# First wave of quantized weights gathered inside the chip's memory in a macaron + S4 kernel

## The chip, the cores and the metric

The kernel runs on one core of one Trainium2 chip. The metric is device time in microseconds (us): the median of three runs of the kernel before is 2035.08 us (2033.29 to 2036.26).

## The reference

The input `u` has 2048 rows of 1024 numbers in float32 (2 sequences of 1024). Three residual blocks follow one another:

```python
x = x + 0.5 * ffn(layernorm(x))
x = x + s4(layernorm(x))
x = x + 0.5 * ffn(layernorm(x))
# ffn, the same weights both times:
h = silu(xf @ Wg) * (xf @ Wu)     # 1024 -> 2752
out = h @ Wd                      # 2752 -> 1024
# each W is dequantized from 4 bits, eight rows of W to a 32-bit word:
w = (w4[k, n] - (z4[k // 128, n] + 1)) * s[k // 128, n]
```

A group is 128 rows of a weight matrix that share a row of zero points and a row of scales; the 1024 rows have eight groups.

## The kernel before, in words

**Work and order.** The tokens go in four blocks of 512. Block and layer make eight jobs (`JOBS`). In each job `gate_up` runs eight waves (`WAVES`), and each of the first five waves makes three blocks of 128 columns of gate and of up at once, in six banks of PSUM (`pg`). A wave takes eight steps, one for each group `g`. A step has twelve products of 512 columns on PE: the weights of the group (`w_up`, float32 made from signed bytes) times a high part `xTh` and a low part `xTl` of the turned input, for each of the six banks. After each step but the last of a wave, each bank is multiplied by the ratio of this group's scale to the next's (`rat`), by ScalarE (ACT, line 811) or VectorE (DVE, line 815): a rescale. The next step adds to the bank, and so waits for it. Steps are numbered through the job: wave 0 is steps 0 to 7, and step 8 is the first of wave 1.

**Weights.** Dequantizing is done once, in job 0. A wave's words (`raw`) are fetched, split into two words of four nibbles each by DVE (`even`, `raw`), added to the zero points spread as bytes, and turned into eight planes of signed bytes (`q`). Plane `j` holds every eighth row of the weights: rows `8r + j`. The planes are written to DRAM (`w_q`), and from there `load_bytes` (line 764) reads a group of 128 rows to the chip (`b`), four steps ahead of use; `make_weights` (line 781) turns it into float32, three steps ahead, on GpSimd (POOL, line 788) for all of wave 0.

**Wave 0** cannot hide this. `first_split` makes its planes. DVE unpacks the zero words (line 351 in eight pieces, line 360 spreads them as `z_w`), and splits the words (lines 591 to 597). POOL makes the odd planes (line 605), ACT the even ones (line 607). Of each plane, the 16 rows of group 0 go from chip to chip into `first_tile` (line 609: eight transfers of 12 KB). The whole planes go to DRAM in four transfers (`keep`, line 613), and groups 1 to 7 are read back from there (line 772).

**The input's first rows.** In `start`, ACT and DVE take the moments of the 512 rows, POOL the power -1/2 (line 205), and DVE refines it (lines 218 to 224). `first_rows` normalizes in pieces: columns 0 to 127, 128 to 511, 512 to 1023, tiles 0 and 2 on DVE, 1 and 3 on ACT. `first_turn(c)` turns column block `c` on PE (four transposes, `pt`) and splits it: ACT copies (line 1829 or 1833), then DVE (1830) or POOL (1834, 1835) makes the low part. Block 0 is turned ahead of step 0, block `c` by step `c`.

**What sets the order.** The instructions of an engine run in the order in which a scheduler put them. `in_order_of_writing` ties those of a stretch of code, on the engines named, to the order in which they were written. Hooks (`at(up, s, f)`) put a piece of work at step `s`, or with `.5` at half of it. Every DMA is issued by an engine's queue (SP, ACT or POOL) in that engine's order, and waits there for its data. `first_weights` (line 716) plans the making of waves 1 to 7 by hooks: at which step a piece of the split (`split`), a plane (`dequantize`, line 660) and a write to DRAM (`keep_bytes`, line 674) go.

**The scales.** `scales_in_pieces` turns rows of scales on PE (`ps_s`), copies them on ACT (line 422), guards them on POOL (lines 425 to 427), inverts them on DVE (line 429) and makes `rat` on POOL (lines 433, 434): for units 0 to 5 in `start`, for units 6 to 17 from step 4 on, and for 18 to 29 from step 6 on.

Of the kernel before, what the change touches and what calls it, by code (L numbers as in the profile page):

```python
# [9 lines left out]
F32 = mybir.dt.float32  # L10
# [47 lines left out]
def macaron_s4_kernel(  # L58
# [270 lines left out]
    def zero_words(which):  # L329

        if which:
            n = HID // 8 // SEGD
            z = t2("zq_1").bitcast(I32)[: GD * SEGD, :n]
            nc.sync.dma_start(z, down_qz.rearrange("g (s n) -> (g s) n", s=SEGD))
            return z
        n = INTER // 8 // SEG
        z = t2("zq_0").bitcast(I32)[:, :n]
        for i, src in enumerate((gate_qz, up_qz)):
            own = slice(GK * SEG * i, GK * SEG * (i + 1))
            nc.scalar.dma_start(z[own], src.rearrange("g (s n) -> (g s) n", s=SEG))  # L340
        return z
# [4 lines left out]

    def unpacked_zeros_in_pieces(tab, z, zi):
# [12 lines left out]
        nc.vector.tensor_scalar(  # L360
            tab.bitcast(U16).rearrange("p (n k) -> p n k", k=2),
            zi.unsqueeze(2).to_broadcast([p, 8 * n, 2]),
            -8.0 * 257,
            120.0 * 257,
            ALU.mult,
            ALU.add,
        )

# [179 lines left out]

    first_tile = bpool.tile([P, width_of(0)], I8, tag="b", name="b_0_0")
    minus_128 = const.tile([P, 1], F32, tag="minus_128", name="minus_128")  # L550
# [7 lines left out]
    def fetch_in_pieces(w, queues=(nc.sync, nc.sync)):  # L558

        raw = t4(f"raw_{w}").bitcast(I32)[:, : width_of(w)]  # L560
        packed[w] = [raw, None]
        for own, i, lo, hi in columns(w):
            queues[i].dma_start(raw[:, own], (gate_qw, up_qw)[i][:, lo:hi])
            yield
# [8 lines left out]
    def first_zero_words():  # L573

        n = width_of(0) // 8
        z = t2("zq_first").bitcast(I32)[:, :n]
        for queue, (own, i, lo, hi) in zip((nc.sync, nc.scalar), columns(0)):
            own = slice(own.start // 8, own.stop // 8)
            src = (gate_qz, up_qz)[i][:, lo // 8 : hi // 8]
            wide = src.unsqueeze(1).to_broadcast([GK, 16, own.stop - own.start])  # L580
            queue.dma_start(z[:, own], wide)
        return z

    def first_split(zq):
# [4 lines left out]
        raw = packed.pop(0)[0]  # L589
        unpacked_zeros(z, zq, zi)  # L590
        nc.vector.tensor_scalar(even, raw, 3, NIBBLES, ALU.logical_shift_left, ALU.bitwise_and)
# [8 lines left out]
        def dequantize(j):  # L600
            pair = pairs.setdefault((j % 2, j // 4), t2(f"q_0_{j}").bitcast(I8)[:, : 2 * n])
            q = pair.rearrange("p (a n) -> p a n", a=2)[:, j // 2 % 2, :]
            view = lambda a, dt: a.bitcast(dt).rearrange("p (n k) -> p k n", k=4)[:, j // 2, :]
            if j % 2:
                nc.gpsimd.tensor_copy(q, view(raw, I8))
            else:
                nc.scalar.activation(q, view(even, U8), AF.Identity, bias=minus_128)
            queue = nc.scalar if j == 6 else nc.sync
            queue.dma_start(first_tile[j:P:8], q[: P // 8])

        def keep(odd, half, queue):
            rows = w_q[0].rearrange("(r b a two) n -> two b r a n", b=2, a=2, two=2)[odd, half]
            queue.dma_start(rows, pairs[odd, half].rearrange("p (a n) -> p a n", a=2))

        return dequantize, keep

# [43 lines left out]
    def dequantize(w, j):  # L660

        n = width_of(w)
        if w not in unpacked:
            q = ypool.tile([P, 4 * TB], F32, tag="y", name=f"q_{w}").bitcast(I8)[:, : 8 * n]
            unpacked[w] = q.rearrange("p (two a n) -> p two a n", two=2, a=4)
        q, src = unpacked[w][:, j % 2, j // 2, :], packed[w][j % 2][:, j // 2, :]
        if w == 1 and j % 2 == 0:
            nc.scalar.activation(q, src.bitcast(U8), AF.Identity, bias=minus_128)
        else:
            nc.gpsimd.tensor_copy(q, src)  # L670
        if j == 7:
            packed.pop(w)

    def keep_bytes(w, odd):
        rows = w_q[w].rearrange("(r a two) n -> two r a n", a=4, two=2)[odd]
        nc.sync.dma_start(rows, unpacked[w][:, odd])

    def fetch_down(a, rt):
# [37 lines left out]
    def first_weights(up, dn, at):  # L716
# [3 lines left out]
        for w in range(1, len(WAVES)):  # L720
            s0 = (0, 4, 8 * w - (14 if w < 5 else 15))[min(w, 3) - 1]
            steps = (0.5, 1, 2.5, 3, 3) if w == 1 else range(6)
            in_pieces(at, [(up, s0 + d) for d in steps], lambda w=w: split(w))
            copies = {1: (3, 3, 3.5, 3.5) + (3.5,) * 4, 2: (3, 3, 4, 4, 5.5, 5.5, 6, 6)}
            copies = copies.get(w, (3, 3, 4, 5, 6, 6, 7, 8))
# [3 lines left out]
            for k, d in zip(EVEN_FIRST, copies):  # L729
                at(up, s0 + d, lambda w=w, k=k: dequantize(w, k))  # L730
            for odd, o in enumerate({1: (3.5, 3.5), 2: (5.5, 7)}.get(w, (6.5, 9.5))):
                at(up, s0 + o, lambda w=w, odd=odd: keep_bytes(w, odd))
# [59 lines left out]
    def next_weights():  # L792
# [4 lines left out]
        for k in range(MAKE) if i == 0 else ():  # L797
            make_weights(k)
        if i + LOAD < len(queue):
            load_bytes(i + LOAD)  # L800
        if i + MAKE < len(queue):
            make_weights(i + MAKE)
        return made.pop(i)


# [11 lines left out]
    def gate_up(j, b, hooks):  # L817
        hi, lo = pieces[b]
        ps = {}
        for s, (wi, g) in enumerate(STEPS):  # L820
# [20 lines left out]
            if j == s == 0:  # L841
                turns = [(1 - k, pos, done) for k, pos, done in turns]
            for i, (k, pos, done) in enumerate(turns):
                if i == len(order):
                    for hook in hooks.get(s + 0.5, ()):
# [20 lines left out]
                if g < GK - 1:  # L866
# [730 lines left out]
    def fast():  # L1597
# [5 lines left out]
        for j, (b, k) in enumerate(JOBS):  # L1603
# [88 lines left out]
            if j == 0:  # L1692
                rows = {}
                for s, f in ((0, lambda: fetch_zeros(1)), (1, lambda: fetch(2)), (2, lambda: fetch_zeros(2))):
                    at(up, s, pinned(f, ET.SP))
# [107 lines left out]
    def first_rows(t, lo, hi):  # L1803
# [39 lines left out]
    def start():  # L1843
# [10 lines left out]
        zeros_down = zero_words(1)  # L1854
        dequantize_first, keep_first = first_split(zq)
        second = fetch_in_pieces(1)
        for j in (1, 3, 5):
            dequantize_first(j)
        next(second)
        dequantize_first(7)  # L1860
        mv, scratch = first_moments()
        dequantize_first(0)
        first_scales = scales_in_pieces(0, 3, srow)
        next(first_scales)
        dequantize_first(2)
        next(first_scales)
        guess(0, 1, mv, LIFT)
        for _ in range(2):
            keep_first(1, _, nc.gpsimd)
        dequantize_first(4)  # L1870
        dequantize_first(6)
        keep_first(0, 1, nc.scalar)
        keep_first(0, 0, nc.sync)
        next(second)
        for _ in first_scales:
            pass
        keep_warm(10, scratch)
# [5 lines left out]
        for t in range(NT):  # L1883
            first_rows(t, 0, P)
        for t in (0, 1, 2):
            first_rows(t, P, 512)
        points = zero_points_in_pieces(0, zeros)
        for _ in range(4):
            next(points)
        first_turn(0)  # L1890
        for _ in range(5):
            next(points)
        first_rows(3, P, 512)
        for t in range(NT):
            first_rows(t, 512, HID)
        for _ in points:
# [93 lines left out]
```

## Time and profile before

| what | us |
|---|---|
| median of three runs | 2035.08 |
| the profiled execution's own time | 2036.95 |
| its span on the core | 2035.2 |
| PE busy in the span | 2004.1 |
| DVE, ACT, POOL busy | 1631.0, 1416.2, 1371.5 |
| first product of step 0 begins | 17.85 |
| the six `xTh` products of step 7 begin | 44.97 |
| the six `xTh` products of step 8 (wave 1) begin | 47.66 |

The span is the stretch of time from the first to the last instruction in the trace; the execution's own time is 1.75 us longer. All times within the run count from the span's start. PE's busy time is an average over all stages: after the first 45 us PE hardly waits, and what the change touches lies in those first 45 us. There the timeline, engine by engine, tells more than the page.

### The profile page before, as it was taken

What the parts mean: (1) busy time and instruction counts of PE and PEld (TensorE: products, weight loads), DVE (VectorE), ACT (ScalarE), POOL (GpSimd) and SP (SyncE); (2) the same over time, 40 slices, a digit from 0 to 9 for tenths busy, and PEclk for the clock granted to TensorE, in tenths of its full rate; (3) what the DMA queues carried; (4) which work ended last, traced back from release to release, by engine and by line L of the source; (5) the groups of instructions that cost most, each with busy time, mean ns of one, the idle gap of its engine ahead of it and who ended that gap; (6) DMA issues with size and microseconds to landing.
All of it is one profiled execution on the core that took longest, in us unless ns stands there. A gap on an engine that the chain in (4) does not pass through costs nothing.

```text
span 2035.2 us, 29665 instructions
## 1 busy us (share of the span) xinstructions
PE 2004.1 (98%) x9202; PEld 1374.5 (68%) x9202; DVE 1631.0 (80%) x2710; ACT 1416.2 (70%) x2221; POOL 1371.5 (67%) x1771
## 2 busy tenths in 40 slices
PE   7999999999999999999999999999999999999998
PEld 4656766577766677656866578667686676866576
DVE  8987878868888778877778777887878878777776
ACT  7888787747775577777767776764776647767775
POOL 6977868748765577655976578754686646965542
PEclk9999999999999999999999999999999999999999
DMA  5343332343524236311552126242263331661113
GB/s 166 119 136 99 110 103 62 79 103 92 148 63 102 73 71 196 120 30 35 143 161 85 33 50 172 79 93 83 50 161 93 84 90 38 160 187 34 35 37 102
DMA packets 345965, 197.13 MB, mean 97 GB/s; under 512 B 166989, under 2 KB 323670, under 8 KB 345798
## 3 DMA queue, kind: packets, MB, share of 16 engines
q1 hardware_dynamic: 344206, 192.55, 34.9%
q10 hardware_dynamic: 1464, 2.20, 0.3%
q8 instruction: 75, 1.23, 0.3%
q14 instruction: 92, 0.75, 0.1%
q0 software_dynamic: 128, 0.39, 0.1%
HBM read 127.52 MB, written 48.57 MB: 87 GB/s over the span
## 4 chain that ended last, share of the span: by engine, by line
PE 93%; DVE 3%; POOL 1%; issue 1%; ACT 1%; DMA 0%; ACTq 0%; POOLq 0%; DVEq 0%
PE pg L855 58%; PE po L949 30%; PE pc L1317 3%; PE pb L1317 1%; ACT pg L811 1%; DVE pg L815 1%; DVE po L815 0%; POOL w_up L788 0%; DVE rawd L629 0%; POOL r L205 0%; DVE hf L890 0%; POOL hl L897 0%; DVE rawd L632 0%; DVE stats L1797 0%; POOL q L670 0%
## 5 line engine op out<-in xcount | busy, mean ns | idle before, releaser
L811 ACT ACTIVATE pg<-pg,rat 128x512 f32<-128x512 f32 x1280 | 807.1, 661 | 383.6 <-PE pg L855 378.8
L815 DVE TENSOR_TENSOR pg<-pg,rat 128x512 f32<-128x512 f32 x1128 | 748.2, 692 | 146.5 <-PE pg L855 139.1
L855 PE MATMUL pg<-xTh,w_up 128*128 128x512 f32 x2752 | 844.4, 435 | 3.9 <-DVE pg L815 2.7
L855 PE MATMUL pg<-xTl,w_up 128*128 128x512 f16 x2752 | 708.0, 381 | 2.5 <-DVE pg L815 2.0
L855 PEld LDWEIGHTS pg<-xTh,w_up 128*128 128x128 f32 x2752 | 518.4, 189 | 167.5 <-DVE pg L815 7.7
L788 POOL CAST w_up<-b 128x768 fp32r<-128x768 int8 (+2 forms) x491 | 376.6, 773 | 356.9 <-PE pg L855 259.1
L811 ACT ACTIVATE po<-po,ratd 128x512 f32<-128x512 f32 x669 | 438.2, 662 | 145.3 <-PE po L949 144.6
L949 PE MATMUL po<-hl,w_down 128*128 128x512 f32 x1344 | 527.5, 393 | 3.5 <-DVE po L815 3.1
L949 PE MATMUL po<-hh,w_down 128*128 128x512 f32 x1344 | 523.4, 390 | 0.0
L815 DVE TENSOR_TENSOR po<-po,ratd 128x512 f32<-128x512 f32 x611 | 424.4, 696 | 112.1 <-PE po L949 111.2
L855 PEld LDWEIGHTS <-w_up 128*128 128x128 bf16 x2752 | 226.7, 98 | 340.2 <-issue 156.1
L788 POOL CAST w_down<-bd 128x512 fp32r<-128x512 int8 x352 | 217.8, 623 | 151.6 <-PE po L949 73.7
L949 PEld LDWEIGHTS po<-hl,w_down 128*128 128x128 f32 x1344 | 252.5, 188 | 64.0 <-DVE po L815 8.3
L949 PEld LDWEIGHTS po<-hh,w_down 128*128 128x128 f32 x1344 | 252.8, 188 | 51.3
L897 POOL TENSOR_TENSOR hl<-hf,hh 128x512 fp32r<-128x512 f32 x168 | 217.1, 1292 | 7.1
L896 POOL CAST hh<-hf 128x512 fp32r<-128x512 f32 x168 | 108.3, 645 | 81.1 <-DVE hf L890 62.3
L890 DVE SCALAR_TENSOR_TENSOR hf<-pg,rat,g 128x512 f32<-128x512 f32 x168 | 121.1, 746 | 40.5 <-ACT g L887 34.3
L887 ACT ACTIVATE g<-pg,rat 128x512 f32<-128x512 f32 x168 | 110.1, 688 | 33.7 <-PE pg L855 17.8
L1002 POOL TENSOR_TENSOR x<-x,yr 128x512 f32<-128x512 f32 x52 | 66.8, 1284 | 0.0
L291 POOL TENSOR_TENSOR lo<-x,hi 128x512 f16<-128x512 f32 x48 | 62.0, 1291 | 0.0
L189 DVE BATCH_NORM_STATS2 stats<-x 128x6 f32<-128x512 f32 x88 | 60.0, 681 | 0.0
L289 POOL TENSOR_TENSOR mid<-hi,top 128x512 bf16<-128x512 f32 x48 | 56.0, 1167 | 0.0
(214 smaller groups left out, 1081.2 us busy)
## 6 DMA issues: line engine op xcount, KB each, us to landing
b<-wq SPq DMA_DIRECT2D x319, 96.0 KB
bd<-wdq SPq DMA_DIRECT2D x336, 64.0 KB
x<-in_L_attn_u_dram SPq DMA_DIRECT2D x30, 512.0 KB
yz<-y SPq DMA_DIRECT2D x56, 256.0 KB
yr<-yz SPq DMA_DIRECT2D x56, 256.0 KB
b<-wq SPq DMA_DIRECT2D x128, 64.0 KB
sz<-xn SPq DMA_DIRECT2D x16, 512.0 KB
st<-sz SPq DMA_DIRECT2D x64, 128.0 KB
```

What stands on the lines that cost most here:

```text
L291: nc.gpsimd.tensor_tensor(lo[:, own], n[:, own], hi[:, own].bitcast(F32), ALU.subtract)
L788: nc.gpsimd.tensor_copy(t, b)
L811: nc.scalar.activation(dst, src, AF.Copy, scale=sc)
L815: nc.vector.tensor_tensor(dst, src, sc.to_broadcast(list(dst.shape)), ALU.mult)
L855: product = lambda: nc.tensor.matmul(p, weights, (lo, hi)[k][:, g, :], start=(g == 0 and not done), stop=(g == GK - 1 and done), skip_grou ...
L887: nc.scalar.activation(g, pg, AF.Silu, scale=rat[:, 2 * f, GK - 1 :])
L890: nc.vector.scalar_tensor_tensor(hf, pu, last, g, ALU.mult, ALU.mult)
L896: nc.gpsimd.tensor_copy(hi, hf)
L897: nc.gpsimd.tensor_tensor(lo, hf, hi.bitcast(F32), ALU.subtract)
L949: nc.tensor.matmul(ps[c], w[:, bass.ts(c, P)], part, start=(f == 0 and k == 0), stop=(f == NF - 1), skip_group_check=True,)
L1002: nc.gpsimd.tensor_tensor(part, part, rows_back.pop((a, t)), ALU.add)
L1317: nc.tensor.matmul(dst, lhsT, rhs, start=start, stop=stop, skip_group_check=True)
```

## The change

The order of instructions from step 9 or so on is the same on every engine; what differs lies ahead of it.

1. **Words by row, then group.** The words of wave 0 lie on the chip with row `r` of group `g` on partition `8r + g` (before: `16g + r`), and the zero words likewise. A plane's 128 partitions thus hold, for each `r`, the eight groups side by side, and one transfer puts them into partition `8r + j` of a tile `landed` (128 x 8 x 768 bytes): eight transfers of 96 KB, in place of eight of 12 KB, four of 192 KB to DRAM, and seven loads of 96 KB. Step 0's weights wait for all eight, and the other groups' for nothing more. `landed` is written to DRAM once, at step 3, for the later jobs.
2. **A plane to POOL, the zero words' last step to ACT.** Plane 0 is a `tensor_scalar` on POOL; the spread of the zero words (before: line 360 on DVE) is an `activation` on ACT.
3. **The rows' second halves** (columns 512 to 1023, four pieces) go from DVE and ACT to POOL, behind the first four `w_up`.
4. **Wave 1** keeps its planes in four tiles of their own (`landed` has the place of `q`), writes them in four transfers of 192 KB where two of 384 KB were, as each pair of planes is done, and spreads splits and planes over later steps. ACT's planes are tied to the order of writing among the rescales. The loads of steps 8 and 9, and `w_up` of step 8, are issued at step 5.5.
5. **Order at the start.** The guard of the scales goes behind the even planes; five pieces of the zero points ahead of the refinement; step 0 does its six `xTh` products ahead of the six `xTl` products, with block 1 turned after three; blocks 2 and 3 are turned half a step or a step later. Rescales are tied to the order of writing in steps 0 to 6. Three loads go from ACT's queue to SP's.

```diff
-            nc.scalar.dma_start(z[own], src.rearrange("g (s n) -> (g s) n", s=SEG))
+            nc.sync.dma_start(z[own], src.rearrange("g (s n) -> (g s) n", s=SEG))
...
-        nc.vector.tensor_scalar(
...
+        if on_act:
+            nc.scalar.activation(dst, src, AF.Copy, bias=120.0 * 257, scale=-8.0 * 257)
+        else:
+            nc.vector.tensor_scalar(dst, src, -8.0 * 257, 120.0 * 257, ALU.mult, ALU.add)
...
-    first_tile = bpool.tile([P, width_of(0)], I8, tag="b", name="b_0_0")
+    landed = ypool.tile([P, 4 * TB], F32, tag="y", name="landed").bitcast(I8)[:, : 8 * width_of(0)]
+    landed = landed.rearrange("p (g n) -> p g n", g=GK)
...
+            if w == 0:
+                src = src.rearrange("(g r) n -> r g n", g=GK)
...
-            if j % 2:
+            if j == 0:
+                nc.gpsimd.tensor_scalar(q, view(even, U8), -128.0, None, ALU.add)
+            elif j % 2:
                 nc.gpsimd.tensor_copy(q, view(raw, I8))
             else:
                 nc.scalar.activation(q, view(even, U8), AF.Identity, bias=minus_128)
             queue = nc.scalar if j == 6 else nc.sync
-            queue.dma_start(first_tile[j:P:8], q[: P // 8])
+            queue.dma_start(landed[j:P:8], q)
...
+    def keep_landed():
+        nc.sync.dma_start(w_q[0].rearrange("(g p) n -> p g n", p=P), landed)
...
-        if j == 7:
+        if j == (6 if w == 1 else 7):
...
+    def keep_half(odd, half):
+        rows = w_q[1].rearrange("(r b a two) n -> two b r a n", b=2, a=2, two=2)[odd, half]
+        nc.sync.dma_start(rows, unpacked.pop((1, odd, half)))
...
-            steps = (0.5, 1, 2.5, 3, 3) if w == 1 else range(6)
+            steps = (1.5, 2, 3, 3.5, 3.5) if w == 1 else range(6)
...
-            copies = {1: (3, 3, 3.5, 3.5) + (3.5,) * 4, 2: (3, 3, 4, 4, 5.5, 5.5, 6, 6)}
+            copies = {1: (3.5, 4, 4.5, 5) + (4,) * 4, 2: (3, 3, 4, 4, 5.5, 5.5, 6, 6)}
...
+                make = lambda w=w, k=k, make=make: in_order_of_writing(make, *STARTING[:1] * (w == 1))
...
+                for odd, half, s in ((0, 0, 4.5), (1, 0, 4.5), (1, 1, 5), (0, 1, 5.5)):
+                    at(up, s, lambda odd=odd, half=half: keep_half(odd, half))
+                at(up, 5.5, late_weights)
...
-        if i == 0:
-            loaded[i] = first_tile
+        if i < GK:
+            loaded[i] = landed[:, i, :]
...
+    LATE = GK, GK + 1
+
+    def late_weights():
+        for i in LATE:
+            load_bytes(i)
+        make_weights(LATE[0])
...
-                turns = [(1 - k, pos, done) for k, pos, done in turns]
+                turns = [(1 - k, pos, k == 1) for k in range(2) for pos in range(len(order))]
...
-                    in_order_of_writing(rescale, *STARTING[:2] * (j == s == 0))
+                    in_order_of_writing(rescale, *STARTING[:2] * (j == 0 and s < 7))
...
-                    at(up, {1: 0.5, 2: 0.5, 4: 2.5}.get(c, c - 2), pinned(more, *STARTING, ET.PE))
+                    at(up, {1: 0.5, 2: 1, 3: 1.5, 4: 2.5}.get(c, c - 2), pinned(more, *STARTING, ET.PE))
+                for t in range(NT):
+                    more = lambda t=t: first_rows(t, 512, HID)
+                    at(up, 0.5, pinned(more, ET.Pool))
...
-        if t % 2:
+        if half:
+            nc.gpsimd.tensor_scalar(n, src, m, r, ALU.subtract, ALU.mult)
+        elif t % 2:
...
-            (nc.sync, nc.scalar)[t % 2].dma_start(x[0][t], src)
+            (nc.scalar if t == 1 else nc.sync).dma_start(x[0][t], src)
```

More of the change, by code (lines that the diff above doesn't have):

```diff
@@ L345, in unpacked_zeros, with unpacked_zeros_in_pieces @@
             pass
-    def unpacked_zeros_in_pieces(tab, z, zi):
+    def unpacked_zeros_in_pieces(tab, z, zi, on_act=False):
         p, n = z.shape
@@ L359, in unpacked_zeros_in_pieces @@
             yield
-        nc.vector.tensor_scalar(
[L361 to L367, printed above, removed]
+        dst = tab.bitcast(U16).rearrange("p (n k) -> p n k", k=2)
+        src = zi.unsqueeze(2).to_broadcast([p, 8 * n, 2])
+        if on_act:
+            nc.scalar.activation(dst, src, AF.Copy, bias=120.0 * 257, scale=-8.0 * 257)
+        else:
+            nc.vector.tensor_scalar(dst, src, -8.0 * 257, 120.0 * 257, ALU.mult, ALU.add)
     def zero_points(which, z):
@@ L562, in fetch_in_pieces @@
         for own, i, lo, hi in columns(w):
-            queues[i].dma_start(raw[:, own], (gate_qw, up_qw)[i][:, lo:hi])
+            src = (gate_qw, up_qw)[i][:, lo:hi]
+            if w == 0:
+                src = src.rearrange("(g r) n -> r g n", g=GK)
+            queues[i].dma_start(raw[:, own], src)
             yield
@@ L579, in first_zero_words @@
             src = (gate_qz, up_qz)[i][:, lo // 8 : hi // 8]
-            wide = src.unsqueeze(1).to_broadcast([GK, 16, own.stop - own.start])
+            wide = src.unsqueeze(0).to_broadcast([16, GK, own.stop - own.start])
             queue.dma_start(z[:, own], wide)
@@ L589, in first_split @@
         raw = packed.pop(0)[0]
-        unpacked_zeros(z, zq, zi)
+        unpacked_zeros(z, zq, zi, True)
         nc.vector.tensor_scalar(even, raw, 3, NIBBLES, ALU.logical_shift_left, ALU.bitwise_and)
@@ L608, in dequantize @@
             queue = nc.scalar if j == 6 else nc.sync
-            queue.dma_start(first_tile[j:P:8], q[: P // 8])
[L611 to L615, printed above, removed]
+            queue.dma_start(landed[j:P:8], q)
+        return dequantize
+    def keep_landed():
+        nc.sync.dma_start(w_q[0].rearrange("(g p) n -> p g n", p=P), landed)
     def signed_bytes(key, raw, even, z, even_signed=True):
@@ L662, in dequantize @@
         n = width_of(w)
[L663 to L666, printed above, removed]
+        src = packed[w][j % 2][:, j // 2, :]
+        if w == 1:
+            if j % 4 < 2:
+                half = t2(f"q_1_{j}").bitcast(I8)[:, : 2 * n]
+                unpacked[1, j % 2, j // 4] = half.rearrange("p (a n) -> p a n", a=2)
+            q = unpacked[1, j % 2, j // 4][:, j // 2 % 2, :]
+        else:
+            if w not in unpacked:
+                q = ypool.tile([P, 4 * TB], F32, tag="y", name=f"q_{w}").bitcast(I8)[:, : 8 * n]
+                unpacked[w] = q.rearrange("p (two a n) -> p two a n", two=2, a=4)
+            q = unpacked[w][:, j % 2, j // 2, :]
         if w == 1 and j % 2 == 0:
@@ L729, in first_weights @@
             for k, d in zip(EVEN_FIRST, copies):
-                at(up, s0 + d, lambda w=w, k=k: dequantize(w, k))
-            for odd, o in enumerate({1: (3.5, 3.5), 2: (5.5, 7)}.get(w, (6.5, 9.5))):
+                make = lambda w=w, k=k: dequantize(w, k)
+                make = lambda w=w, k=k, make=make: in_order_of_writing(make, *STARTING[:1] * (w == 1))
+                at(up, s0 + d, make)
+            if w == 1:
+                for odd, half, s in ((0, 0, 4.5), (1, 0, 4.5), (1, 1, 5), (0, 1, 5.5)):
+                    at(up, s, lambda odd=odd, half=half: keep_half(odd, half))
+                at(up, 5.5, late_weights)
+                continue
+            for odd, o in enumerate({2: (5.5, 7)}.get(w, (6.5, 9.5))):
                 at(up, s0 + o, lambda w=w, odd=odd: keep_bytes(w, odd))
@@ L798, in next_weights @@
             make_weights(k)
-        if i + LOAD < len(queue):
+        if i + LOAD < len(queue) and i + LOAD not in LATE:
             load_bytes(i + LOAD)
-        if i + MAKE < len(queue):
+        if i + MAKE < len(queue) and i + MAKE != LATE[0]:
             make_weights(i + MAKE)
         return made.pop(i)
+    LATE = GK, GK + 1
[3 more added lines that the diff above has]
+        make_weights(LATE[0])
     h = {}
@@ L841, in gate_up @@
             if j == s == 0:
-                turns = [(1 - k, pos, done) for k, pos, done in turns]
+                turns = [(1 - k, pos, k == 1) for k in range(2) for pos in range(len(order))]
             for i, (k, pos, done) in enumerate(turns):
-                if i == len(order):
+                if i == len(order) // (1 + (j == s == 0)):
                     for hook in hooks.get(s + 0.5, ()):
@@ L1693, in fast @@
                 rows = {}
-                for s, f in ((0, lambda: fetch_zeros(1)), (1, lambda: fetch(2)), (2, lambda: fetch_zeros(2))):
+                for s, f in ((0, lambda: fetch_zeros(1)), (1, lambda: fetch(2)), (2, lambda: fetch_zeros(2)), (3, keep_landed)):
                     at(up, s, pinned(f, ET.SP))
@@ L1854, in start @@
         zeros_down = zero_words(1)
-        dequantize_first, keep_first = first_split(zq)
+        dequantize_first = first_split(zq)
         second = fetch_in_pieces(1)
-        for j in (1, 3, 5):
+        for j in (1, 3, 5, 7):
             dequantize_first(j)
         next(second)
-        dequantize_first(7)
         mv, scratch = first_moments()
-        dequantize_first(0)
+        for j in (0, 2, 4, 6):
+            dequantize_first(j)
+        next(second)
+        guess(0, 1, mv, LIFT)
         first_scales = scales_in_pieces(0, 3, srow)
         next(first_scales)
-        dequantize_first(2)
         next(first_scales)
[L1867 to L1876, printed above, removed]
+        points = zero_points_in_pieces(0, zeros)
+        for _ in range(5):
+            next(points)
         keep_warm(10, scratch)
@@ L1884, in start @@
             first_rows(t, 0, P)
-        for t in (0, 1, 2):
+        for _ in first_scales:
+            pass
+        for t in (0, 2, 1):
             first_rows(t, P, 512)
-        points = zero_points_in_pieces(0, zeros)
-        for _ in range(4):
+        for _ in range(3):
             next(points)
         first_turn(0)
-        for _ in range(5):
-            next(points)
         first_rows(3, P, 512)
-        for t in range(NT):
-            first_rows(t, 512, HID)
         for _ in points:
```

## The prediction

> **What bounds the kernel now.** I read the page first: the chain that ended last is PE's, and PE's idle time is what a change can win.
>
> ```profile
> PE 2004.1 (98%) x9202; PEld 1374.5 (68%) x9202; DVE 1631.0 (80%) x2710; ACT 1416.2 (70%) x2221; POOL 1371.5 (67%) x1771
> ...
> PE 93%; DVE 3%; POOL 1%; issue 1%; ACT 1%; DMA 0%; ACTq 0%; POOLq 0%; DVEq 0%
> ```
>
> PE is idle for 31.1 us (2035.2 less 2004.1), and most of that lies ahead of the first product or at the end. So I read the windows view of the stages next; its columns are the window, its length, then busy time and count of PE, PEld, DVE, ACT, POOL, the granted clock, the DMA share and GB/s.
>
> ```profile
> 17.85:24.00 6.15, 5.26 (x29) 3.56 (x30) 5.35 (x15) 5.26 (x9) 1.91 (x3) 1.00 0.58 187
> 24.00:30.00 6.00, 5.83 (x30) 3.46 (x29) 5.14 (x10) 4.12 (x7) 4.55 (x5) 1.00 0.58 185
> 30.00:36.00 6.00, 5.87 (x31) 3.35 (x28) 5.93 (x8) 5.91 (x10) 5.08 (x5) 1.00 0.23 67
> 36.00:42.00 6.00, 5.55 (x29) 3.27 (x30) 4.26 (x7) 5.43 (x11) 5.53 (x11) 1.00 0.40 131
> ```
>
> In the first window PE idles 0.9 us while POOL does 1.9 us of 6; later DVE and ACT are full (5.9 of 6). Third, the timeline (start, duration, instruction, idle time before with its releaser):
>
> ```profile
> 16.90 0.81 POOL L788 CAST w_up<-b 128x768 fp32r<-128x768 int8 x1
> 17.85 0.94 PE L855 MATMUL pg<-xTh,w_up 128*128 128x512 f32 x3 [0.17 <-POOL w_up L788]
> 22.09 3.47 POOL L788 CAST w_up<-b 128x768 fp32r<-128x768 int8 x4 [4.38 <-DMA b<-wq]
> ```
>
> POOL waits 4.38 us for the trip through DRAM. Last, the chain of waits in order of time: further on it is no longer that trip which holds PE.
>
> ```profile
> 35.41 3.42 POOL q L670 x4
> ...
> 40.43 0.75 DVE safe L429
> ...
> 41.51 0.70 DVE pg L815
> 42.20 0.04 issue
> ```
>
> Wave 1's planes hold up the guard of the scales on POOL, that holds the reciprocal on DVE, and a rescale stands behind it.
>
> **The most there is to win.** Steps without stalls are 2.69 us apart (the six `xTh` products begin at 42.27, 44.97, 47.66). Step 8 begins at 47.3: of the six `xTl` products from 46.54, three are step 7's, 0.25 each. Steps 0 to 7 are 8 x 2.69 = 21.5, seven turns of four transposes 7 x 0.55 = 3.9 (0.60 for four, overlapping), twelve small scale transposes 1.1: 26.5 us. From 17.85 that ends at 44.3. So at most 47.3 - 44.3 = 3.0 us, 0.15% of the time, as later steps keep their order and run back to back (PE busy 20.00 of 20 us from 60 on).
>
> **Ahead of the first product.** Taken from DVE: the spread `z_w`, 0.96 (line 360). It wins nothing: the next DVE instruction, at 5.30, waited for the words, whose DMA ends the chain at 5.28. On ACT it starts behind the warm activation, which ends at 4.87. ACT took 1.06 for 1024 columns and 0.66 for 512, which gives 1.46 for 1536: done at 6.35, and DVE wants it at 6.49. Cover 0.15 us; if it takes 2 us instead, 0.4 is lost. The words land on 128 partitions as before, so I cost their new order at nothing; no work hides it, and each 0.1 us by which they land later is lost at once. Three loads move to SP's queue: the rows' last tile, wanted by DVE at 11.66 (DMA traffic drops near 10), and the zero points' words, wanted near 13.4. The scale rows behind them landed at 10.77 and are now wanted by ACT near 13.6: cover 2.8 us.
>
> Plane 0 on POOL stands between the odd planes (end 11.9) and the power of line 205, which began at 13.41 when its input came. No row shows a `tensor_scalar` of this width. Low end: a copy of it, 0.82. High end: POOL's `tensor_scalar` rows, 0.345 at 48 columns and 0.466 at 104, so 2.16 ns a column and 1.9 us. I take 1.9, being the same operation: end 13.85, power 0.45 late. At 0.82 it hides in the idle time.
>
> Behind the power, POOL now does the guard of the scales (three instructions, 12.08 to 13.15 before, covered by idle time; ScalarE's input for it is now ready near 13.9), then waits for DVE's reciprocal (0.45), then `rat` (0.8, from 433 and 434), then `w_up`. Removed there: two DMA issues, 14.41 to 16.13. So: power to 14.9, guard to 15.95, reciprocal to 16.65 (behind five small DVE instructions and two pieces of rows), `rat` to 17.5, `w_up` to 18.35, first product 18.4. At the low price 18.0. The planes must have landed by 17.5: SP issues planes 0, 2, 4 from 13.9 at 0.55 each, the last at 15.0. The load of 96 KB that released POOL at 22.09 was issued at 19.69: 2.4 us. So 17.4, cover 0.1. I take the start as **0.55 us later**, between 0.15 and 1.1.
>
> **Steps 0 to 2.** Before, step 0 took until 23.09 to give way to step 1, with blocks 1 to 3 turned. Now, one after the other: three fp32 products twice (0.94 each, as at 17.85, since nothing overlaps them), six fp16 products 1.5, two turns 1.1, together 4.5: step 1 at 22.9, with block 3 (0.55) still to turn. Nothing is won here: the wait for DRAM is gone, but the later start and the turn in the way are late next. Step 3 then begins at 22.9 + 2 x 2.69 + 3 x 0.55 = 29.95; before, 29.99.
>
> The four row pieces taken from DVE (2 x 0.5) and ACT (2 x 0.8) relieve both at 18 to 20 us, where PE waited for neither. On POOL a piece costs between a cast of 512 columns, 0.62, and 1.35 by the slope above; I take 1.35: after four `w_up` (17.5 to 20.8) they end at 26.2, and the turn of block 4 wants them at 27.4. Cover 1.2 us. Block 3's low part then ends at 29.7 on POOL, needed at 29.95: cover 0.25.
>
> DVE did the same 512 columns in 0.54 each (1.00 for two). [...]
>
> **Steps 3 to 8.** DVE does the last two steps of wave 1's split (1.0 to 1.68 and 0.57) behind the rescale of step 3, at 32.1: done at 34.4 (before 34.72). POOL's four planes (3.42) run to 37.8, guard to 39.05 (1.25 less one instruction moved ahead), reciprocal to 39.85, a split piece 0.5, rescale 0.7: 41.1, against 42.20. PE wants that bank at 40.3, so **this stall stays, some 0.8 us**. Before, two of step 6's products (0.5) had been done when it began; now, by the order of instructions, the stalled bank comes first. Step 6 then runs 41.1 to 44.0, with 0.2 us of waiting for ACT, step 7 to 46.7. Before: 47.3. Won: 0.6.
>
> New wait: `w_up` of step 8. ACT's last plane stands behind rescales, tied in that order. Per step ACT has three or four rescales (0.66), a copy (0.6) and up to two planes (0.92) in 3.2 us: the last plane ends near 40.5, its write is issued until 41.1. Before, the last write was issued until 39.4 and the load at 41.84: 2.4; then 2.4 to land and 0.83 to convert: 46.7. No cover. Behind SP's load wait further loads, and behind POOL's conversion wave 2's planes, which PE needs 20 us later. I put 0.1 of loss here. The DRAM write of `landed` (768 KB, step 3) lies in a window at 67 GB/s and nobody waits for it.
>
> **Sum.** 0.6 less 0.1 is 0.5 us won: 2036.95 - 0.5 = 2036.45 for an execution like the profiled one, which was 1.87 above the median; from the median, 2035.08 - 0.5 = **2034.6**.
>
> **Rivals.** (A) The forecast: -1.2 to +0.2 us. For it: the chain above, and ACT full. Chance 0.50.
>
> (B) The win comes through: POOL's `tensor_scalar` costs like a copy, so PE starts at 18.0, and ACT and DVE, relieved, let no chain form. Wave 0 ends at 18.0 + 26.5 + 0.7 (step 0 took 4.5 above, against 2.69 and two turns) = 45.2, that is -2.1: 2033.0; range -1.2 to -3.0. Against it: reciprocal and planes keep their order. Chance 0.22.
>
> (C) Slower: wave 1's bytes come late. Place: the load of step 8, behind ACT's last plane. Price: each us by which this plane ends past 40.5 is a us at step 8. It decides from 41.1, where the win is used up; planes ending at 42.5 give 48.7, +1.4: 2036.5. For it: ACT was 5.91 of 6 busy, and the plan moves these planes one step back. Against it: ACT is 1.6 us freer early. Over 0.2% it would take 45.2. Chance 0.18.
>
> (D) The change does not do what it says: with all eight planes behind one wait, the transfers to 16 partitions land near 19 and the start slips by 2 us, about what the trip's removal gives: +0.2 to +1.5. Chance 0.10.
>
> **How the numbers follow.** A measurement of this kernel can tell some 0.2%, 4.1 us, from no change, and the bound on the win is 3.0 us; so faster by more needs something I do not see: 0.04. Slower by more takes the far end of C or D: 0.05. Within: 0.91. The range: -2.6 from B, +2.0 from C and D, about the forecast, and the medians' own spread (2033.29 to 2036.26 in three runs): 2032.2 to 2037.0.
>
> **What would show it.** Right: POOL's 4.4 us wait for `b` gone; first product at 18.0 to 18.9; step 3 begins near 30; the rescale behind the reciprocal ends near 41; step 8 begins at 46 to 47. Wrong: a first product ahead of 17.8 or past 19.5; PE waiting for POOL's `w_up` at step 8 by over 1 us; a difference in the time that arises behind step 8, where I see none.

## The result, and the profile after

In 22 runs of each kernel taken side by side the kernel before has a median of 2036.01 us (2032.37 to 2038.27) and the changed kernel 2040.03 (2036.25 to 2043.16). The ratio is 1.0017, with a 95% interval of 1.001 to 1.0023: the change makes the kernel some 3.5 us slower. That is within 0.2%, but on the other side of the forecast 2034.6 and 3 us above the top of its range. The profiled execution of the changed kernel took 2040.49 us, its span 2038.7.

First the page of the changed kernel, the engines' busy time and the chain that ended last.

```profile
PE 2005.8 (98%) x9202; PEld 1376.3 (68%) x9202; DVE 1627.4 (80%) x2707; ACT 1415.0 (69%) x2219; POOL 1381.8 (68%) x1774
...
PE 92%; POOL 3%; DVE 2%; issue 1%; ACT 1%; DMA 1%; SPq 0%; POOLq 0%; DVEq 0%; ACTq 0%
```

POOL is busy 10.3 us more than before, and its share of the chain goes from 1% to 3% (DVE's from 3% to 2%): the path moved from DVE to POOL. Next the windows of the same stages, with the columns as before (PE, PEld, DVE, ACT, POOL, granted clock, DMA share, GB/s).

```profile
17.85:24.00 6.15, 6.15 (x30) 4.41 (x30) 4.33 (x11) 3.77 (x7) 6.15 (x7) 1.00 0.21 63
24.00:30.00 6.00, 4.88 (x25) 3.02 (x22) 4.67 (x8) 4.41 (x8) 6.00 (x4) 1.00 0.64 192
30.00:36.00 6.00, 5.08 (x18) 3.30 (x19) 3.39 (x5) 2.24 (x4) 5.91 (x7) 0.72 0.48 154
36.00:42.00 6.00, 6.00 (x37) 3.83 (x35) 5.97 (x9) 5.92 (x11) 5.92 (x7) 1.00 0.10 33
```

POOL is full in all four stages; in the first it had 1.91 us of work before. From 24 to 36, PE, DVE and ACT all wait. The granted clock falls to 0.72 in the third stage. (PE's 6.15 in the first row is no gain: it counts the warming transposes ahead of the first product.) The timeline of the start (start, duration, instruction, idle time before with its releaser) shows where POOL's work comes from:

```profile
12.54 2.14 POOL L607 TENSOR_SCALAR q<-even_w 128x768 int8<-128x768 uint8 x1
...
17.71 0.34 POOL L431 TENSOR_TENSOR rat<-s_gu,safe 128x42 f32<-128x42 f32 x1 [0.97 <-DVE safe L427]
...
18.44 3.50 POOL L810 CAST w_up<-landed 128x768 fp32r<-128x768 int8 x4
...
19.39 1.57 PE L884 MATMUL pg<-xTh,w_up 128*128 128x512 f32 x3
```

The wait of 4.38 us for `b` on POOL is gone, as the change means it to: the second to fourth `w_up` follow the first at once. But the first product begins at 19.39 instead of 17.85. And then POOL alone (the last row, wave 1's planes, answers to 35.37 before):

```profile
21.93 8.93 POOL L1844 TENSOR_SCALAR xn<-x,mv,r 128x512 f32<-128x512 f32 x4
...
39.61 3.46 POOL L681 COPY q<-raw 128x768 int8<-128x768 int8 x4
```

The four row pieces hold POOL for 8.93 us, 2.2 each, until 30.9. PE's own timeline shows who waits for them:

```profile
28.17 0.38 PE L1861 MATMUL pt<-ident,xn 128*128 128x128 f32 x2
28.87 0.33 PE L1861 MATMUL pt<-ident,xn 128*128 128x128 f32 x1 [0.32 <-POOL xn L1844]
30.92 0.45 PE L1861 MATMUL pt<-ident,xn 128*128 128x128 f32 x1 [1.73 <-POOL xn L1844]
31.03 1.63 PE L884 MATMUL pg<-xTh,w_up 128*128 128x512 f32 x3
```

The turn of block 4 has two of its four tiles at 28.2; the third comes 0.32 and the fourth 1.73 us late. Behind it three products take 1.63 us where three took 1.05 at 27.29. The windows of one us each say why (the window, its length, then PE busy, granted clock, DMA share, GB/s):

```profile
30.00:31.00 1.00, 0.08 (x1) 0.99 0.91 265
31.00:32.00 1.00, 1.00 (x3) 0.50 1.03 347
...
33.00:34.00 1.00, 1.00 (x5) 0.50 0.22 74
34.00:35.00 1.00, 1.00 (x8) 0.80 0.00 0
```

After the stall PE runs for about 3.4 us at half its clock. Last the chain of waits in order of time (start, us, what):

```profile
24.01 6.86 POOL xn L1844 x3
30.87 1.55 POOL w_up L810 x2
...
39.67 3.39 POOL q L681 x4
...
44.42 0.10 DVE safe L427
...
45.59 0.61 DVE pg L844
46.20 0.04 issue
```

It is the old chain (planes of wave 1, guard, reciprocal, rescale) with the row pieces in front: POOL never gets rid of the delay, and the rescale that ended at 42.20 ends at 46.20. Step 8's six `xTh` products begin at 52.15 instead of 47.66: 4.5 us late. From there on the two traces keep that distance (4.4 us at 300 us, 3.9 at 1000, 4.5 at 2020, each read at the same product by its count); behind PE's last work the rest of the changed kernel is 0.9 us shorter in this profile (8.3 us against 9.2), so that the spans differ by 3.5.

### The profile page after: what moved, and what is told of

Same layout as the page of the kernel before. It is cut to its first block, busy times and chain, and to the rows that moved or that the text cites. A ratio compares the mean times of both kernels' runs of the same rounds, so it can differ in the third digit from the quotient of the medians.

```text
span 2038.7 us, 29656 instructions
## 1 busy us (share of the span) xinstructions
PE 2005.8 (98%) x9202; PEld 1376.3 (68%) x9202; DVE 1627.4 (80%) x2707; ACT 1415.0 (69%) x2219; POOL 1381.8 (68%) x1774
## 3 DMA queue, kind: packets, MB, share of 16 engines
q10 hardware_dynamic: 1008, 1.54, 0.2%
## 4 chain that ended last, share of the span: by engine, by line
PE 92%; POOL 3%; DVE 2%; issue 1%; ACT 1%; DMA 1%; SPq 0%; POOLq 0%; DVEq 0%; ACTq 0%
PE pg L884 57%; PE po L978 29%; PE pc L1346 3%; PE pb L1346 1%; POOL w_up L810 1%; DVE pg L844 1%; ACT pg L840 1%; POOL xn L1844 0%; DVE po L844 0%; POOL r L205 0%; POOL qd L719 0%; DMA raw<-_L_ffn_gate_qweight_dram 0%; POOL hl L926 0%; DVE rawd L633 0%; DVE rawd L636 0%
## 5 line engine op out<-in xcount | busy, mean ns | idle before, releaser
L810 POOL CAST w_up<-b 128x768 fp32r<-128x768 int8 (+2 forms) x483 | 368.5, 769 | 352.1 <-PE pg L884 258.8
```

The costliest lines, as they stand in the source:

```text
L810: nc.gpsimd.tensor_copy(t, b)
```

## The experiments

"A" is the changed kernel, "B" the kernel before. Step 8 is read as before, by its six `xTh` products. Line numbers shift by a few lines from kernel to kernel.

**rows_back: A, with the row pieces on DVE and ACT again.**

```diff
-        if half:
-            nc.gpsimd.tensor_scalar(n, src, m, r, ALU.subtract, ALU.mult)
-        elif t % 2:
+        if t % 2:
...
-                for t in range(NT):
-                    more = lambda t=t: first_rows(t, 512, HID)
-                    at(up, 0.5, pinned(more, ET.Pool))
...
         first_rows(3, P, 512)
+        for t in (1, 3):
+            first_rows(t, 512, HID)
         for _ in points:
             pass
+        for t in (0, 2):
+            first_rows(t, 512, HID)
```

> The changed kernel, but the rows' second halves are made by VectorE and ScalarE again, ahead of step 0. Theory (GpSimd's tensor_scalar: four row pieces took 8.9 us there, held the turn of block 4 for 2 us, let PE's clock fall to half and made all later GpSimd work late): the stall at block 4 and the low clock are gone, the six xTh products of step 8 begin at 48.3 to 49.3 us (52.15 with the change), and the time is 2.5 to 4 us below the changed kernel's, 0 to 1.5 us above before's. Rival (the new plan of wave 1 and the tied rescales make the stall behind the reciprocal): the rescale behind the reciprocal still ends near 46 us and the time stays within 1 us of the changed kernel's.

Measured: median 2032.19 (11 runs), beside 2037.03 for B; ratio 0.9981 [0.9972, 0.999]. In the profile step 8 begins at 47.26, the granted clock is 1.00 in all windows of the start, and PE's waits (us in total, times, longest) no longer name `xn` on POOL:

```profile
PE pg L884 <- DVE pg L844: 0.9, 2, 0.7
PE pt L1856 <- DVE xn L1843: 0.7, 1, 0.7
PE pg L884 <- ACT xn L1841: 0.7, 1, 0.7
```

In A the first row of that view is `PE pt L1861 <- POOL xn L1844: 2.0, 2, 1.7`. So taking back one part out of five undoes the loss: step 8 comes 4.9 us earlier than in A and 0.4 us earlier than in B. The lead over B in the times is larger than that, some 4 us; the runs' own spread, below, comes back to it.

**plane0_back: A, with plane 0 on ACT again.**

```diff
-            if j == 0:
-                nc.gpsimd.tensor_scalar(q, view(even, U8), -128.0, None, ALU.add)
-            elif j % 2:
+            if j % 2:
```

> The changed kernel, but plane 0 is made by ScalarE again; the row pieces stay on GpSimd. Theory: GpSimd's 2.14 us before the power of line 205 go, of which 0.8 us stood on the path: first product at 18.4 to 18.8 us (19.39 with the change); the stall at block 4 stays some 2 us and moves forward by as much; step 8's six xTh products at 51.0 to 51.6, time 0.5 to 1.2 us below the changed kernel's. Rival (the first product waits for the planes' landing or for the later words, not for GpSimd): first product stays at 19.2 or later and the time is unchanged.

Measured: 2039.17 (11 runs), ratio to B 1.0008 [0.9999, 1.0017]. POOL now idles 1.59 us ahead of the power, the first product comes at 19.05 (0.34 earlier), block 4's turn still waits 1.73 us for the fourth piece, the clock still falls, and step 8 begins at 51.47: plane 0 is worth 0.7 us there. The four pieces take 8.59 us. In this execution the words came 0.25 us later than in A's (6.14 against 5.89), so the plane's own price at the first product is nearer 0.6 (0.34 + 0.25).

**both_back: A, with both undone.**

> The changed kernel with both the row halves and plane 0 off GpSimd. Theory: the two add up, first product 18.4 to 18.8, step 8's six xTh products at 47.3 to 48.3 (before 47.66), time within 1 us of before's, 3 to 4.5 us below the changed kernel's. Rival (plan of wave 1 or the words' order cost as much): still 2 us or more above before's.

Measured: 2033.88 (9 runs), ratio 0.9978 [0.9968, 0.9988]. First product at 18.58. The end of the chain of waits:

```profile
34.24 3.45 POOL q L679 x4
...
39.05 0.75 DVE safe L427
...
40.13 0.70 DVE pg L842
40.83 0.04 issue
```

The old chain is there, 1.4 us earlier than in B, and step 8 begins at 46.78, 0.9 us earlier. What is left of the change (the single transfers into one tile, the new plan of wave 1, the order at the start and the zero words on ACT) wins 0.9 us at step 8, and of these parts only the last is taken apart, in zeros_on_vector: from the first product to step 3 it takes 10.8 us (18.58 to 29.36), where B takes 12.1 (17.85 to 29.99) and A 15.1 (19.39 to 34.51). In the medians this version beats both kernels; how much of that is work saved is asked below.

**kept_warm: A, with transposes without use on PE in the stall.**

```diff
+        if c == 4:
+            keep_warm(4)
         ps = bank(f"pt_0_1_{c}")
         for t in range(NT):
+            if c == 4 and t == 3:
+                keep_warm(12)
             src = first[t, c // 4][:, bass.ts(c % 4, P)]
```

> The changed kernel with 16 transposes more, into a bank that nobody reads, in the two waits of PE at the turn of block 4, so that PE is hardly idle there. It tells what the low clock costs beside the wait itself. If the clock matters: granted clock 1.00 in 30 to 36 us (0.72 with the change), step 3 begins at 32.8 to 33.5 (34.51), and as GpSimd's planes wait for a scale transpose on PE, step 8 is 0.5 to 1.8 us earlier and the time lower by as much. If GpSimd alone holds the path: step 3 is earlier, but step 8 and the time stay within 0.3 us.

Measured: 2041.55 (11 runs), ratio to B 1.0021 [1.0011, 1.003]: not faster than A. The clock stays at 1.00, step 3 comes 0.76 us earlier than in A (33.75 against 34.51), and then PE waits 0.83 us for POOL's low part and 1.69 us for the rescale; step 8 begins at 52.25, as in A. The row pieces and the product that the rescale holds up:

```profile
21.64 8.59 POOL L1844 TENSOR_SCALAR xn<-x,mv,r 128x512 f32<-128x512 f32 x4
45.62 0.38 PE L884 MATMUL pg<-xTl,w_up 128*128 128x512 f16 x1 [1.69 <-DVE pg L844]
```

From the end of the pieces (30.23) to that product it takes 15.4 us, and in A, at half clock, 15.4 too (30.86 to 46.24). So the half clock is a consequence and not the loss: POOL's queue ends the path with or without it. That step 8 is equal as well is in part chance: the product is 0.6 us earlier than in A, since the pieces ended so much earlier, and the lead is gone by step 8. With the transposes POOL's order came out different there: `rat` stands ahead of the first `w_up` of step 8, and PE waits 0.27 us for it.

**rows_alone: B, with only the row pieces moved to POOL.**

> The kernel before with one part of the change alone: the four rows' second halves go to GpSimd at step 0.5 of the products; planes, words, zero words and wave 1's plan stay as they were. Theory (GpSimd pays some 2.2 us for each of these pieces, and everything behind them on its queue is late): four pieces of about 2.2 us, 8.8 in all, from about 20.4 on with w_up casts between them, so the last one ends near 29.3 to 30.5; block 4's turn waits 0.5 to 2 us for it on TensorE, wave 1's planes and the guard go back by 2 to 4 us, the six products of step 8 begin at 50 to 51.5 (47.66 before), and the time is 2 to 4 us over the kernel before. Rival (the late words and plane 0 are the loss, the pieces are covered): step 8 at 47.7 to 48.2, and the time within 1 us of the kernel before.

Measured: 2042.76 (8 runs), beside 2036.05 for B; ratio 1.0032 [1.0021, 1.0043]: 6.5 us slower, and worse than I expected and than A itself. POOL's timeline shows why:

```profile
22.35 2.69 POOL L788 CAST w_up<-b 128x768 fp32r<-128x768 int8 x3 [4.44 <-DMA b<-wq]
25.04 8.27 POOL L1815 TENSOR_SCALAR xn<-x,mv,r 128x512 f32<-128x512 f32 x4
```

In B the pieces stand behind `w_up` that wait for DRAM. I had them start at 20.4; they start at 25.0, and three transposes wait for them, 4.4 us in all. By the count of products step 8 is 6.8 us late. The four pieces take 8.27 us here, 2.07 each. The rival, that the pieces were covered and the late words the loss, is out.

**price_list: A, and behind it single operations on POOL at the very end.** Three of each; the list is extra work, and its time says nothing.

```diff
+                nc.gpsimd.tensor_copy(pb, pa)
+                nc.gpsimd.tensor_scalar(pb, pa, 2.0, None, ALU.add)
+                nc.gpsimd.tensor_scalar(pb, pa, 2.0, 3.0, ALU.subtract, ALU.mult)
+                nc.gpsimd.tensor_scalar(pb, pa, pm, pm, ALU.subtract, ALU.mult)
+                nc.gpsimd.tensor_tensor(pb, pa, pa, ALU.add)
...
+                nc.gpsimd.tensor_copy(pd, src_)
+                nc.gpsimd.tensor_scalar(pd, src_, -2.0, None, ALU.add)
```

> The changed kernel with a list of single GpSimd operations put at the very end, where no other engine has much left to do; the list is extra work and its result is not used. Theory (a tensor_scalar costs GpSimd this much whatever runs beside it): the form of the rows' halves (512 f32, two operations, both scalars per partition) takes 1.9 to 2.2 us, about the same as with one operation, and over three times a copy of the same size (0.6); 768 uint8 with one operation takes 1.9 to 2.2 where the copy takes 0.8. Rival (the pieces were stretched because VectorE was busy beside them): 0.6 to 1.2 us for 512 f32 and 0.8 to 1.2 for 768 uint8.

Measured, groups of POOL by line and form (count, busy us, mean ns, idle before); L1822 to L1826 are the five of the first block in order, L1833 and L1834 the copy and the operation on bytes:

```profile
L1834 POOL TENSOR_SCALAR price_d<-price_c 128x768 int8<-128x768 uint8 x3 | 6.4, 2122 | 0.1
L1825 POOL TENSOR_SCALAR price_b<-price_a,price_m 128x512 f32<-128x512 f32 x3 | 6.2, 2069 | 0.0
L1824 POOL TENSOR_SCALAR price_b<-price_a 128x512 f32<-128x512 f32 x3 | 5.7, 1920 | 0.0
L1823 POOL TENSOR_SCALAR price_b<-price_a 128x512 f32<-128x512 f32 x3 | 4.4, 1488 | 0.0
L1825 POOL TENSOR_SCALAR price_b<-price_a,price_m 128x256 f32<-128x256 f32 x3 | 3.6, 1214 | 0.0
...
L1823 POOL TENSOR_SCALAR price_b<-price_a 128x256 f32<-128x256 f32 x3 | 2.5, 847 | 0.0
L1833 POOL CAST price_d<-price_c 128x768 int8<-128x768 uint8 x3 | 2.5, 820 | 0.1
...
L1822 POOL COPY price_b<-price_a 128x512 f32<-128x512 f32 x3 | 1.8, 603 | 0.0
```

DVE's last instruction ends at 2040.6 and most of the list runs behind it, until 2080: the piece's form costs 2.07 us with nothing beside it. The rival, that DVE's work beside it stretched the pieces, is out; what else runs beside it can explain at most the step from 2.07 to the 2.2 seen in A. With immediates, one operation instead of two saves 0.43 (not "about the same", as I had expected); an immediate instead of a scalar per partition saves 0.15. (The operation on bytes reads every second byte here; plane 0 reads every fourth.)

**words_order_alone: B, with the words of wave 0 and the zero words by row and group as in A.**

```diff
+            if w == 0:
+                src = src.rearrange("(g r) n -> r g n", g=GK)
...
-            wide = src.unsqueeze(1).to_broadcast([GK, 16, own.stop - own.start])
+            wide = src.unsqueeze(0).to_broadcast([16, GK, own.stop - own.start])
```

> The kernel before, but wave 0's packed words and their zero words lie row by row of all groups on the partitions instead of group by group. The rest isn't changed with them, so planes and groups no longer belong together: other weights are multiplied than the reference asks for, and the kernel is only for the time at which the words land. Theory (the order of the rows makes the transfer land later): VectorE's first use of the words (even_w) begins at 5.8 to 6.0 instead of 5.30, and the first product at 18.3 to 18.5 instead of 17.85. Rival (something else delays them, such as the zero words' transfer on another queue): 5.3 and 17.85.

In this kernel planes and groups no longer belong together, so that only its times mean something. Measured, one profiled execution (2037.09), its first use of the words on DVE beside B's (the second row):

```profile
5.92 0.56 DVE L594 TENSOR_SCALAR even_w<-raw 128x768 int32<-128x768 int32 x1 [0.44 <-DMA raw<-_L_ffn_gate_qweight_dram]
5.30 0.56 DVE L591 TENSOR_SCALAR even_w<-raw 128x768 int32<-128x768 int32 x1
```

The first product begins at 18.56, and step 8 is 0.5 us late. In the three profiles of kernels with B's order the first use comes at 5.30, 5.50 and 5.56, with no wait shown; in the thirteen with A's order it lies between 5.56 and 6.56, 5.89 in the middle, each time behind the words' transfer. So the order of the rows delays the first use of the words by some 0.4 us in the middle, by 0.6 between the two profiles compared here, with a spread of up to a us among the thirteen. What in the transfer takes longer is open.

**zeros_on_vector: both_back, with the zero words' last step on DVE again.**

> The changed kernel without rows' halves and plane 0 on GpSimd, and with the zero words' last step on VectorE again, so that only the new transfers and the new plan of wave 1 are left. Theory (the step on VectorE stands ahead of the planes by its own length, 0.5 to 0.8 us, of which late words hide nothing): the planes and the first product come 0.3 to 0.8 us later than in the same kernel with the step on ScalarE (18.58). Rival (VectorE waits for the words anyway and the step is hidden): the first product within 0.15 us of 18.58.

Measured, one profiled execution (2034.98): the step takes DVE 0.96 us from 4.40 to 5.36, and DVE then waits 1.20 us for the words, which come at 6.56 here. The step is hidden; the first product at 19.41 is late by the words. The words' spread is larger than the 0.15 us that I had set as the limit, so the first product itself decides nothing; the wait behind the step does. Counted from the first use of the words, the first product comes 12.85 us later here and 12.92 in both_back, so that moving the step wins nothing that shows.

**The runs' own spread.** One thing did not fit. Rows_back beats B by 4 us in the times and by 0.4 us at step 8. The runs of most of these kernels lie in two groups, some 3 to 4 us apart: rows_back near 2031.5 and 2035, B mostly near 2036.5 with a few at 2032.5. The profiles of B and A both have a second half-clock stretch (0.50 from 250 to 252 us in B, from 254 to 256 in A), behind a stall near 245 us that the change does not touch (2.47 us up to 247.81 in B, 2.44 up to 252.22 in A); in kept_warm's profile (2037.81, of its lower group) it is missing: the clock is 1.00 up to 258 us, behind a stall of 2.24. So I filled that stall with transposes in three kernels: B, A and both_back.

```diff
             for c in range(4):
+                if (j, d, c) == (0, 30, 1):
+                    keep_warm(16)
```

> The kernel before with 16 transposes without use on TensorE just ahead of the product of the first down-projection that waits some 2.5 us for VectorE near 245 us; nothing of the start is touched. Theory (the runs of every kernel here fall in two groups some 3 to 4 us apart, because this stall is or isn't followed by 3.4 us at a granted clock of 0.50, and the change moves only the share of the two): the clock stays at 1.00 past 250 us, the runs lie in one group near the lowest ones of the kernel before (2031 to 2034), and the median falls by 2 to 4 us. Rival (the groups have another cause, such as the tail or the transfers): the median within 1 us of the kernel before and the same two groups.

> The changed kernel with the same 16 transposes at the same product. Theory: one group near the lowest runs of the changed kernel (2036 to 2038), and over the kernel before with the stall filled by the 4.5 us that the profiles show at step 8, give or take 1. Rival: the median stays near 2040, in two groups.

> The changed kernel without rows' halves and plane 0 on GpSimd, with the same 16 transposes at the same product. Theory: one group near the lowest runs of the kernel without the fillers (2030 to 2032), 0.5 to 2 us under the kernel before with the stall filled, since step 8 begins 0.9 us earlier; of the 4 us by which it beat the kernel before, the rest was the share of the two groups. Rival (the new transfers are worth those 4 us themselves): 3 to 5 us under the kernel before with the stall filled.

Measured, 11 runs each: B 2035.53 (2033.86 to 2037.25), A 2038.71 (2037.44 to 2040.27), both_back 2035.00 (2034.14 to 2036.16); ratios to B unchanged 0.9996 [0.9987, 1.0005], 1.0014 [1.0005, 1.0023] and 0.9994 [0.9985, 1.0003]. The clock stays at 1.00 past 250 us and the runs of each lie closer together, but not at the level of the lowest runs: against the medians without filling B gains 0.7 us, A 1.3, and both_back loses 1.1. (The unfilled medians were not all taken side by side with the filled ones: B, 2036.20 here, was at 2036.01 beside A and at 2037.03 beside both_back.) The expectation is half right. With the stall filled, A is 3.2 us slower than B (2038.71 - 2035.53), and both_back's 0.5 us of lead is not clear of the runs' spread. That agrees with step 8 in these three profiles (48.03, 51.79 and 47.11, so 3.8 and 0.9), and not with the 3 us and more by which both_back beats B unfilled. What it wins beyond 1 us is thus a larger share of low runs and not work saved at the start. For rows_back, 0.4 us ahead of B at step 8, the same is likely, but it was not run with the stall filled. Their lead over A, 4.9 and 5.4 us at step 8, is work saved.

Three more profiles were to catch a low run:

> The changed kernel with the rows' second halves back on VectorE and ScalarE, looked at again for an execution of its lower group (2031 to 2032; the first look at 2035.43 was of the upper one). Theory (a half clock near 250 us comes or stays away): in an execution near 2031 the clock is 1.00 past 250 us, and TensorE is 1.5 to 2.5 us ahead of the first look from 256 us on; the rest lies in the tail. Rival (the stall of 2.47 us before it is missing as well, because VectorE's 3.14 us operation is short there): 4 us ahead from 256 us on.

> As the look before it: an execution near 2031 tells by how much TensorE is ahead at 256 us (1.5 to 2.5 us by the clock alone, 4 us if the stall is missing as well); one near 2035 repeats the first look.

> The changed kernel with both parts back on VectorE and ScalarE, looked at again for an execution of its lower group (2030 to 2031; the first look was at 2036.04). The same two readings as for the looks before it: 1.5 to 2.5 us ahead at 256 us by the clock alone, 4 us if the stall of 2.2 us before it is missing as well.

Measured: 2034.19, 2034.86 and 2034.82; none is a low run. But in the first the half clock stayed away (1.00 from 244 to 254 us) though the stall was there (2.1 us). From 244 to 256 us PE gains 1.8 us on B's profile in it, and 0.2 in the second, where the half clock came (behind the stall two rescales on DVE lie 1.70 us apart there, at 248.67 and 250.37, and 0.93 in the first, at 248.40 and 249.33): it costs about 1.7 us here (the product that B begins at 244.15 and the one at 255.90, found in each trace by its count). The other 2 us of the lower group remain **open**. The one profile from a lower group, kept_warm's, has a span 2.8 us under A's: 1.6 arise between 244 and 256 us, and 0.5 behind PE's last work. That last stretch takes 7.7 to 9.4 us in the profiles (9.2 in B, 8.3 in A, 7.8 in rows_back), so that part of the difference between runs may lie there; what sets its length was not tried.

## Why the prediction was wrong

**The step that failed** is the price of a row piece: "On POOL a piece costs between a cast of 512 columns, 0.62, and 1.35 by the slope above; I take 1.35", "Cover 1.2 us". It measured 2.07 alone and 2.2 in place. Four make 8.9 us and not 5.4. From their true start, 21.93, pieces of 1.35 would have ended at 27.3, ahead of the 28.2 at which the turn wants them; at 2.2 they ended at 30.9, 2.7 us past it. Of the 4.7 us by which they end later than forecast (26.2), the price is 3.5 and the later start 1.1. Even in the forecast's own sum, four pieces of 2.07 from 20.8 on end at 29.1, past the 27.4 at which it needed them. The upper end was no bound. I drew it through two rows of 48 and 104 columns that have one operation and an immediate; the piece has two operations and two scalars per partition. The price list gives 2.5 ns a column for the first form ((1488 - 847) / 256) and 3.3 for the second ((2069 - 1214) / 256).

**What stands behind it** I had seen but not charged: POOL's queue carries the low parts, wave 1's planes and the guard, and the chain of before already ran through them. A delay on POOL there has no slack: 4.2 us at the planes (35.37 to 39.61) became 4.0 at the rescale and 4.5 at step 8. The half clock behind the stall I did not foresee; by kept_warm it costs nothing on the way to the rescale.

**The start**: 19.39, forecast 18.4, outer end 18.95. The words' new order, which I cost "at nothing", cost about 0.6 us (words_order_alone: 0.7 at the first product). Plane 0, taken at 1.9, took 2.14; the price list gives 2.12, so my slope nearly held for that form. Counted from the first use of the words, the first product comes after 12.55 us in B, 12.91 in plane0_back and 13.50 in A: of the 1.54 us that the start is late, 0.59 are the words, 0.59 plane 0, and the other 0.36 lie in the rest of the change, where the forecast's sum had 0.55 for everything. As forecast, late words were lost at once.

**Right**: the zero words on ACT (1.46 forecast, 1.48 measured, cost nothing; winning nothing, as zeros_on_vector shows), the wait for DRAM gone, and the chain from the planes on. In rows_back, where the pieces alone are taken back, the rescale ends at 41.3 (forecast 41.1) and step 8 comes 0.4 us earlier than in B (forecast 0.6 less 0.1). There was luck in it: the first product, at 19.07, is 0.7 later than forecast, and from there to step 3 it takes 10.8 us instead of 11.55 (18.4 to 29.95), so that two misses cancel.

**The rivals**: B is refuted by the price list. C did not happen: `w_up` of step 8 is converted from 49.92 on in A, and PE does not wait for it; nor does it in both_back, where POOL is not late and the conversion begins at 44.55. D, planes landing late, did not happen: no wait for their landing shows ahead of the first `w_up`. None of the four held the mechanism that came: I named POOL's price with a cover of 1.2 us, and gave it no rival of its own.

## What to carry to other kernels

Ahead of moving work to an idle engine, price the very form of instruction there, with its operations and kinds of scalars, and follow the whole queue behind it: idle time in the window's average is not idle time at the place. A bound drawn from rows of another form is no bound. And where runs lie in groups, compare profiles at a fixed mark beside the medians, or take the cause of the groups out of both kernels.

## What the runs showed of the hardware

- GpSimd's `tensor_scalar` on 128x512 f32 took (price_list) 1.49 us with one operation, 1.92 with two and 2.07 with two and scalars per partition; a copy took 0.60, a `tensor_tensor` 1.03. On 768 bytes with one operation it took 2.12, a copy 0.82.
- A stall of 2.1 to 2.5 us of PE near 245 us was followed by 3.4 us at a granted clock of 0.50 in most profiles without filling and not in others, at the same place of the same kernel: rows_back had it behind 2.47 us, its second profile had none behind 2.14, and plane0_back had it behind 2.14. What decides between the two was not shown.
- VectorE's `tensor_scalar` on 88x1024 uint16 took 0.41 us at 238.95 and 3.14 at 244.01 in B. PE's wait of 2.47 us near 245 us ends with the rescale that stands behind the long one. The first began in a pause of 0.08 us between two GpSimd instructions, the second beside a row of them without a pause (five, from 243.91 to 247.6). Whether this row stretches it was not tried.
